# Attention weights turned through two buffers: large query tiles at the end of a turn with transfers of their own, small ones in the next

## The chip, the cores and the metric

The kernel runs on one core of one Trainium2 chip. The metric is the device time of one execution in microseconds (us). PE is the matrix engine (TensorE), PEld its weight loads, DVE is VectorE, ACT ScalarE, POOL GpSimd, and SP is SyncE, which here issues nearly all DMAs.

## What is computed

The reference is a block of three residual steps on an input of 16 batches, 512 tokens and width 256. The first and the last step are a feed-forward part with routed slots, and the middle one, which the change touches, is causal self-attention with 16 heads of width 64 and rotary positions:

```python
x = x + 0.5 * ffn(layernorm(x))
x = x + attn(layernorm(x))
x = x + 0.5 * ffn(layernorm(x))

def attn(x):
    q, k, v = heads(x @ Wq + bq), *heads(split(x @ Wkv + bkv))
    q, k = rope(q), rope(k)
    scores = where(causal, q @ k.T / sqrt(64), -inf)
    return concat(softmax(scores) @ v) @ Wo + bo
```

All is float32.

## The kernel before

Attention works in 64 units: a batch `b` and a group `hg` of four heads. A loop over `u` (L1207) makes one **turn** per step, and each turn works on several units at once: `sums(u)` and `leave(u)` finish unit `u`, `old` is unit `u+1`, whose softmax weights are scaled and turned, `new` is unit `u+2`, whose scores and exponentials are made, and `queries_keys(u+3)` makes the next queries and keys. All engines' orders within attention are written out by hand: every engine runs its instructions in the order in which the loop's calls stand, so a wait of one instruction holds all that stand behind it on the same engine. SP's DMA issues are in this order too.

The 512 queries of a unit are four tiles of 128 (0 to 3). Because of the causal mask, tile `i` has `i+1` blocks of 128 x 128, ten in all. Scores come in three groups: `scores((3,))`, `scores((2,))` early in a turn, `scores((1, 0))` at its end. `exps` (L1061) follows each group: on VectorE a masked copy out of PSUM with the row's minimum (L1073), on ScalarE the exponential with the row's sum (L1077). `scaled` (L1080) takes reciprocals of the sums on VectorE (L1082) and multiplies on POOL (L1085). The weights of tiles 3 and 2 lie in one SBUF tile, `pr0` (7 blocks per head), those of 1 and 0 in another, `pr1` (3 blocks).

To multiply by the values, the weights must stand with their keys on the partitions. This is done in two steps. `turn` (L1088, L1100) transposes every 32 x 32 square of a block on VectorE, from `pr` into `sq`. Then `move` (L1119, L1127) issues 16 DMAs on SP that bring each band of 32 partitions of `sq` to its place in `prT`. `sq` and `prT` are one buffer each: `sq` can be written again when the 16 DMAs have read it, and `prT` when `sums` have read it. `turn_most(j)` turns six of the seven blocks of tiles 3 and 2 for head `j`, `turn_corner` the last one for all heads, `turn_tile(1)` and `turn_tile(0)` the small tiles. For the first unit and the last, `turn_at_once` does the whole on PE instead.

`sums` (L1149, L1158) multiplies: for each pair of heads and each key block `t`, one matmul per head over the `4 - t` query tiles that see it, accumulated in a PSUM bank (`p_av`) that ScalarE then copies to `aoT` (L1169). `leave` (L1171) multiplies by Wo and VectorE adds to the residual (L1182). The q and k products (L988) are biased and rotated on VectorE (L994) and POOL (L999, L1000); `values` makes v (L1010).

In every fourth turn a new batch is entered: ScalarE normalizes it (`enter`, L936), VectorE transposes it (L961), and a `Trip` stores it to DRAM on SP (L964). In the two turns after that, `land` issues eight DMAs each on SP (L970) that read it back turned. In these turns SP also stores a finished batch (L1184, two DMAs).

PSUM has eight banks that go around: in a turn `sums` takes two, scores of tile 3 four, of tile 2 four, `leave` two, q, k and v two each, scores of tiles 1 and 0 four. So the third and fourth head of `scores((2,))` use the banks that the two `p_av` leave, and each group of scores starts with small matmuls of a blank tile (L1047) that are first to wait for a bank.

In a turn of the kernel before, the order around the change is: `sums`; `enter` and `land` where there are any; `scaled` of `old`'s tiles 1 and 0 for two heads, `turn_most(1)`, `turn_most(2)`, `scaled` for the other two heads, `turn_most(3)`, `turn_corner`, `turn_tile(1)`; `scores((3,))`, `scores((2,))`; the exps of tile 3's first head; `turn_tile(0)` and `move`; the other exps; `leave`; statistics, q, k and v; `scores((1, 0))`, `turn_most(0)`, `exps((1, 0))`.

Of the kernel before, what the change touches and what calls it, by code (L numbers as in the profile page):

```python
# [9 lines left out]
F32 = mybir.dt.float32  # L10
# [5 lines left out]
P = 128  # L16
NB, S, D = 16, 512, 256
NT = S // P
# [15 lines left out]
AH, DQ = 16, 64  # L34
HG = 4
NHG = AH // HG
SQ = 32
NSQ = P // SQ
# [9 lines left out]
def macaron_kernel(ctx: ExitStack, tc: tile.TileContext, a: dict, out: bass.AP):  # L48
    nc = tc.nc
# [6 lines left out]
    def ps(name):  # L56
        return psum.tile([P, 512], F32, tag="b", name=name, bufs=8)
# [22 lines left out]
    ident = const.tile([P, P], F32, tag="ident", name="ident")  # L80
# [83 lines left out]
    with tc.tile_pool(name="setup", bufs=1) as su:  # L164
# [3 lines left out]
        sq = su.tile([NS, D], F32, tag="sq", name="sq")  # L168
# [7 lines left out]
        with tc.manual_schedule(engines={mybir.EngineType.DVE, mybir.EngineType.Activation}):  # L176
            pt = ps("p_sqT")
# [20 lines left out]
            for c in range(NC):  # L198
                for k in range(NC):
                    nc.tensor.matmul(pq[:, c * NS:(c + 1) * NS], d_wq[:, k, c * P:(c + 1) * P], sqT[:, k, :],  # L200
                                     start=(k == 0), stop=(k == NC - 1))
# [683 lines left out]
    def attention(qp, wq, wk, wv, wo, cos, sin, row):  # L885


        ap = None
# [23 lines left out]
        hTs, hs, qs, ks, vs, oTs, prTs, stds, trips = {}, {}, {}, {}, {}, {}, {}, {}, {}  # L912
# [30 lines left out]
        def width(b):  # L943
            hTs[b] = qp.tile([P, NC, S], F32, tag="hT", name=f"ahT{b}", bufs=2)
            for c in range(NC):
                pt = ps(f"p_ahT{b}_{c}")
                for t in range(NT):
                    nc.tensor.transpose(pt[:, t * P:(t + 1) * P], hs[b][t // 2][:, t % 2, c * P:(c + 1) * P], ident)
                nc.scalar.copy(hTs[b][:, c, :], pt)  # L949
# [65 lines left out]

        blocks = NT * (NT + 1) // 2
        first = [0, 4, 8, 7]
        place = {0: (1, 0, 1), 1: (1, 1, 2), 2: (0, 0, 3), 3: (0, 3, 4)}  # L1020

        class Weights:

# [2 lines left out]
            def __init__(self, u):  # L1026
                b, hg = units[u]
                self.u, self.hg, self.nm = u, hg, f"{b}_{hg}"
                self.mn = small.tile([P, NT, HG], F32, tag="amn", name=f"amn{self.nm}")
                self.rs = small.tile([P, NT, HG], F32, tag="ars", name=f"ars{self.nm}")  # L1030
                self.pr = [None, None]
                self.banks = {}

            def at(self, i, j):
# [53 lines left out]
            def turn(self, which, heads, of, src, dst):  # L1088

                if heads[0] == 0 and which == 0 and len(of) == 2:
                    self.sq = ap.tile([P, NSQ, HG, blocks * SQ], F32, tag="sq", name=f"sq{self.nm}")
                pr = self.pr[which]

                def view(x, at, dims):
                    return bass.AP(x.tensor, x.offset + at, [list(x.ap[0])] + [[s, n] for s, n in dims if n > 1])
                j, nh = heads
                step = (7, 3)[which] * P
                nc.vector.transpose(  # L1100
                    view(self.sq, j * blocks * SQ + dst[0] * SQ,
                         [(blocks * SQ, nh)] + [(s * SQ, n) for s, (_, n) in zip(dst[1:], of)]
                         + [(HG * blocks * SQ, NSQ), (1, SQ)]),
                    view(pr, j * step + src * P,
                         [(step, nh)] + [(s * P, n) for s, n in of] + [(SQ, NSQ), (1, SQ)]))

            def turn_most(self, j):
                self.turn(0, (j, 1), [(3, 2), (1, 3)], 0, (2, 1, 3))

            def turn_corner(self):  # L1110
                self.turn(0, (0, HG), [], 6, (first[3],))

            def turn_tile(self, i):
                if i:
                    self.turn(1, (0, HG), [(1, 2)], 1, (1, 3))
                else:
                    self.turn(1, (0, HG), [], 0, (0,))

            def move(self):  # L1119

                prT = prTs[self.u] = ap.tile([P, NSQ, HG, blocks * SQ], F32, tag="prT", name=f"prT{self.nm}")
                for n in range(NSQ):
                    for k in range(NSQ):
                        q = (k + n) % NSQ
                        nc.sync.dma_start(prT[k * SQ:(k + 1) * SQ, q, :, :], self.sq[q * SQ:(q + 1) * SQ, k, :, :])  # L1127

            def turn_at_once(self, tag, vector):


                prT = prTs[self.u] = ap.tile([P, NSQ, HG, blocks * SQ], F32, tag=tag, name=f"prT{self.nm}")
                where = {first[t] + i - t: (i, t) for i in range(NT) for t in range(i + 1)}
                per = S // P
                for g in range(HG * blocks // per):
                    pt = ps(f"p_prT{self.nm}_{g}")
                    for n in range(per):
                        j, at = divmod(g * per + n, blocks)
                        i, t = where[at]
                        nc.tensor.transpose(pt[:, n * P:(n + 1) * P], self.at(i, j)[:, t * P:(t + 1) * P], ident)  # L1140
                    dst = prT.rearrange("p a h f -> p a (h f)")[:, :, g * per * SQ:(g + 1) * per * SQ]
                    dst = dst.rearrange("p a (n x) -> p a n x", n=per)
                    src = pt.rearrange("p (n a x) -> p a n x", n=per, a=NSQ)
                    if g in vector:
                        nc.vector.tensor_copy(dst, src)
                    else:
                        nc.scalar.copy(dst, src)

        def sums(u, pair):  # L1149
            b, hg = units[u]  # L1150
            if pair == 0:
                oTs[u] = ap.tile([P, HG // 2, S], F32, tag="oT", name=f"aoT{b}_{hg}")
            po = ps(f"p_av{b}_{hg}_{pair}")
            for t in range(NT):
                n = NT - t
                for j in range(2):
                    head = pair * 2 + j
                    nc.tensor.matmul(  # L1158
                        po[j * DQ:(j + 1) * DQ, :].rearrange("d (a f) -> d a f", a=NSQ)[:, :, t * SQ:],
                        vs[u][:, t, head * DQ:(head + 1) * DQ],  # L1160
                        prTs[u][:, :, head, first[t] * SQ:(first[t] + n) * SQ],
                        start=(t == 0), stop=(t == NT - 1))

            r = R_BV + hg * (HG // 2) + pair
            dst = oTs[u][:, pair, :].rearrange("d (i o a y) -> d o a i y", i=NT // 2, o=2, a=NSQ)
            src = po.rearrange("d (a i o y) -> d o a i y", i=NT // 2, o=2, a=NSQ)
            for odd, to, of in ((1, slice(0, 4), slice(0, 4)), (0, slice(2, 4), slice(0, 2)),
                                (0, slice(0, 2), slice(2, 4))):
                nc.scalar.activation(dst[:, odd, to], src[:, odd, of], AF.Identity, bias=bcol[:, r:r + 1])  # L1169
# [31 lines left out]
        ap = yield [lambda: width(0)] + queries_keys(0)  # L1201
        ws = {}
        seen = 2 * NHG
        with tc.tile_pool(name="awayh", bufs=2, space=bass.MemoryType.DRAM) as away, \
                tc.manual_schedule(engines={mybir.EngineType.DVE, mybir.EngineType.Activation,
                                            mybir.EngineType.Pool, mybir.EngineType.SP}):
            for u in range(-2, nu):  # L1207
                new = ws[u + 2] = Weights(u + 2) if u + 2 < nu else None
                qk = queries_keys(u + 3)
                old = ws.get(u + 1)  # L1210
# [10 lines left out]
                if u >= 0:  # L1221
                    sums(u, 0)
                    sums(u, 1)
# [6 lines left out]
                if old and u + 2 == nu:  # L1230
                    old.turn_at_once("sq", range(0, 10, 2))
                elif u == -1:
                    values(0, 0)
                    values(0, 2)
                    old.turn_at_once("prT", range(2, 10, 3))
                elif old:
                    old.scaled((1, 0), slice(0, HG // 2))
                    old.turn_most(1)
                    old.turn_most(2)
                    old.scaled((1, 0), slice(HG // 2, HG))  # L1240
                    old.turn_most(3)
                    old.turn_corner()
                    old.turn_tile(1)
                if new:
                    new.scores((3,))
                    new.scores((2,))
                    new.exps((3,), slice(0, 1))
                if old and 0 <= u < nu - 2:
                    old.turn_tile(0)
                    old.move()  # L1250
                if new:
                    new.exps((3,), slice(1, 2))
                gone = [leave(u, 0)] if u >= 0 else []
                if fresh == 1:
                    width(1)
# [18 lines left out]
                if u == nu - 1:  # L1274
                    for g in range(PB):
                        entered[g] = xs[g]
                        for t in range(NT):
                            i = (g % PB) * NT + t
# [17 lines left out]
                if new and u > -2:  # L1296
                    new.scores((1, 0))
                    if u + 3 < nu:
                        new.turn_most(0)
                    new.exps((1, 0))  # L1300
            token_stats(NB - 2, NT - 1)
        yield
# [54 lines left out]
```

## Time and profile before

| | us |
|---|---|
| median of three runs | 2309.89 (2309.47 to 2314.15) |
| the profiled execution | 2317.09 |
| its span, first to last instruction | 2315.4 |
| of which attention's steady turns | 476.5 to 1881.8, 60 turns |
| PE busy in the span | 2254.7 (97%) |
| VectorE busy | 1761.6 (76%) |
| all 992 issues of L1127, median of one | 0.59 |

The profile is one execution. An engine is busy while it runs an instruction; an SP row gives the time that SP takes to issue a DMA, not the time that the DMA takes. In a timeline's rows the first number is the start, the second the time from the start of the first to the end of the last of equal neighbours, then engine, line, operation, the tiles written and read, the count, and in brackets the idle time before it and what ended it. A group of matmuls shows twice as many records as the program has matmuls, since one in float32 runs as two. The granted clock of PE was 0.995 over the span.

### The profile page before, as it was taken

How to read it: one execution, taken by the hardware profiler on the slowest of the kernel's cores; microseconds unless marked ns; L12 is line 12 of the kernel's file. 1: busy time of each engine (PE TensorE's matmuls, PEld its weight loads, DVE VectorE, ACT ScalarE, POOL GpSimd, SP SyncE). 2: the span in 40 equal slices, each digit the busy share in tenths (PEclk: the TensorE clock that was granted, in tenths of full speed). 3: DMA queues.
4: the chain of work that ended last, by engine and by line, in shares of the span. 5: the costliest groups of instructions: out<-in, count | busy, mean ns of one | idle time of the engine just before them, and what ended most of it. 6: DMA issues, size and time to landing. Idle time of an engine off the chain costs nothing. (4 is left out here: it accounts for less than half of the span.)

```text
span 2315.4 us, 52884 instructions
## 1 busy us (share of the span) xinstructions
PE 2254.7 (97%) x19544; PEld 1488.2 (64%) x19544; DVE 1761.6 (76%) x4678; ACT 1158.1 (50%) x3296; POOL 1068.6 (46%) x1695
## 2 busy tenths in 40 slices
PE   7999999999999999999999999999999999998999
PEld 4764488566666666666666666666666666764588
DVE  5742298788889898989898988989888875432387
ACT  5753243455555555556464545555555555532233
POOL 2210054565566556565656565656556542210043
PEclk9999999999999999999999999999999999999999
DMA  6839851055556465554655554646455543739734
GB/s 209 261 112 403 339 140 55 7 131 121 130 127 147 110 148 130 122 140 111 146 129 129 128 140 111 158 97 160 120 132 130 124 115 112 237 138 404 305 116 140
DMA packets 221929, 359.52 MB, mean 155 GB/s; under 512 B 99876, under 2 KB 159848, under 8 KB 213480
## 3 DMA queue, kind: packets, MB, share of 16 engines
q1 hardware_dynamic: 220812, 355.34, 55.3%
q8 instruction: 155, 2.54, 0.5%
q14 instruction: 102, 0.84, 0.1%
q10 hardware_dynamic: 860, 0.81, 0.1%
HBM read 156.29 MB, written 37.22 MB: 84 GB/s over the span
## 5 line engine op out<-in xcount | busy, mean ns | idle before, releaser
L1085 POOL TENSOR_SCALAR pr<-pr,ars 128x512 f32<-128x512 f32 (+3 forms) x1024 | 524.1, 532 | 575.0 <-DVE ars L1082 573.8
L1077 ACT ACTIVATE pr<-pr,amn 128x512 f32<-128x512 f32 (+3 forms) x1024 | 561.8, 550 | 219.6 <-DVE amn L1073 215.2
L1100 DVE STREAM_TRANSPOSE sq<-pr 128x768 f32<-128x768 f32 x434 | 384.5, 918 | 130.1 <-DMA prT<-sq 106.7
L1073 DVE CUSTOM_DVE_ANT_0 pr<-p_as,causal 128x512 f32<-128x512 f32 (+2 forms) x768 | 308.6, 457 | 7.0 <-PE p_as L1054 5.8
L1054 PE MATMUL p_as<-k,q 32*64 32x448 f32 (+3 forms) x8192 | 307.3, 414 | 0.0
L1158 PE MATMUL p_av<-prT,v 128*64 128x512 f32 (+3 forms) x2048 | 291.5, 437 | 10.1 <-ACT pr L1077 2.0
L1013 ACT COPY v<-p_v 128x512 f32<-128x512 f32 x128 | 74.6, 585 | 451.3 <-PE p_v L1010 451.3
L1158 PEld LDWEIGHTS p_av<-prT,v 128*64 128x64 f32 x2048 | 161.1, 137 | 139.6 <-issue 92.7
L1176 PE MATMUL p_ay<-wo,aoT 128*128 128x256 f32 x1024 | 238.6, 386 | 4.1 <-DVE amn L1073 3.0
L1010 PE MATMUL p_v<-wv,ahT 128*128 128x256 f32 x1024 | 231.6, 379 | 0.7 <-DVE x L1182 0.7
L988 PE MATMUL p_q<-ahT,wq 128*128 128x512 f32 x512 | 230.6, 593 | 0.2 <-ACT ahT L949 0.2
L1054 PEld LDWEIGHTS p_as<-k,q 32*64 32x64 f32 x8192 | 201.8, 131 | 45.0 <-issue 26.2
L988 PE MATMUL p_k<-ahT,wk 128*128 128x512 f32 x512 | 230.3, 592 | 0.0
L1176 PEld LDWEIGHTS p_ay<-wo,aoT 128*128 128x128 f32 x1024 | 189.2, 190 | 62.2 <-DVE amn L1073 37.0
L1010 PEld LDWEIGHTS p_v<-wv,ahT 128*128 128x128 f32 x1024 | 194.5, 190 | 53.8 <-issue 23.7
L1077 ACT ACTIVATION_READ_ACCUMULATOR pr<-pr,amn 128x1 f32 x1024 | 192.0, 187 | 0.0
L988 PEld LDWEIGHTS p_k<-ahT,wk 128*128 128x128 f32 x512 | 97.3, 190 | 122.0 <-issue 106.9
L988 PEld LDWEIGHTS p_q<-ahT,wq 128*128 128x128 f32 x512 | 97.0, 190 | 95.7 <-issue 78.6
L1073 DVE CUSTOM_DVE_ANT_1 pr<-p_as,causal 128x384 f32<-128x384 f32 x256 | 130.2, 546 | 0.0
L1169 ACT ACTIVATE aoT<-p_av,bcol 128x128 f32<-128x128 f32 (+1 forms) x384 | 117.1, 391 | 9.9 <-PE p_av L1158 9.9
L584 PE MATMUL p_ds<-hT,qk 128*128 128x512 f32 x256 | 118.8, 609 | 2.1 <-ACT hT L159 2.1
L811 PE MATMUL p_cy<-vw,catT 128*128 128x256 f32 x512 | 120.8, 379 | 0.0
(179 smaller groups left out, 3358.0 us busy)
## 6 DMA issues: line engine op xcount, KB each, us to landing
prT<-sq SPq DMA_DIRECT2D x992, 160.0 KB
w<-in_e_W_dram SPq DMA_DIRECT2D x64, 1024.0 KB
w<-in_e_Wg_dram SPq DMA_DIRECT2D x32, 1024.0 KB
out_dram<-x SPq DMA_DIRECT2D x64, 256.0 KB
awaya<-sqa SPq DMA_DIRECT2D x25, 512.0 KB
atT<-awaya SPq DMA_DIRECT2D x100, 128.0 KB
xl<-in_attn_x_dram SPq DMA_DIRECT2D x16, 512.0 KB
xl<-out_dram SPq DMA_DIRECT2D x16, 512.0 KB
```

What stands on the lines that cost most here:

```text
L584: nc.tensor.matmul(psc, qk[:, k, c * P:(c + 1) * P], hT[:, k, :], start=(k == 0), stop=(k == NC - 1))
L811: nc.tensor.matmul(py[:, t * D:(t + 1) * D], atT[:, c, t * P:(t + 1) * P], vws[b][:, c, :], start=(c == 0), stop=(c == NC - 1))
L988: nc.tensor.matmul(pq, self.w[:, k, at:at + P], hTs[self.b][:, k, :], start=(k == 0), stop=(k == NC - 1))
L1010: nc.tensor.matmul(pv[:, t * 256:(t + 1) * 256], hTs[b][:, k, (t0 + t) * P:(t0 + t + 1) * P], wv[:, k, hg * HG * DQ:(hg + 1) * HG * DQ], s ...
L1054: nc.tensor.matmul(banks[j][half * H:(half + 1) * H, at:at + wh], q[n][rows, q0:q0 + H], k[n][rows, :wh], start=(n == 0), stop=(n == 1))
L1073: nc.vector.tensor_tensor_reduce(out=by_block(self.at(i, j)), in0=by_block(banks[j][:, at:at + w]), in1=mask(i), scale=-1.0 / math.sqrt(DQ ...
L1077: nc.scalar.activation(self.at(i, j), self.at(i, j), AF.Exp, bias=self.mn[:, i, j:j + 1], scale=-1.0, accum_out=self.rs[:, i, j:j + 1])
L1085: nc.gpsimd.tensor_scalar(self.at(i, j), self.at(i, j), self.rs[:, i, j:j + 1], 1.0, ALU.mult, ALU.mult)
L1100: nc.vector.transpose(view(self.sq, j * blocks * SQ + dst[0] * SQ, [(blocks * SQ, nh)] + [(s * SQ, n) for s, (_, n) in zip(dst[1:], of)] + ...
L1158: nc.tensor.matmul(po[j * DQ:(j + 1) * DQ, :].rearrange("d (a f) -> d a f", a=NSQ)[:, :, t * SQ:], vs[u][:, t, head * DQ:(head + 1) * DQ], ...
L1169: nc.scalar.activation(dst[:, odd, to], src[:, odd, of], AF.Identity, bias=bcol[:, r:r + 1])
L1176: nc.tensor.matmul(py[:, t * D:(t + 1) * D], oTs[u][:, pair, (t0 + t) * P:(t0 + t + 1) * P], wo[:, hg * (HG // 2) + pair, :], start=(pair ...
```

## The change

The turned weights get two buffers, `sq0`/`prT0` for tiles 3 and 2 (7 blocks per head) and `sq1`/`prT1` for tiles 1 and 0 (3 blocks per head), of the same size together. All of `turn_most` and `turn_corner` now stand at the end of the turn in which tiles 3 and 2 were made, ahead of `exps((1, 0))`; the tiles 1 and 0 are turned in the next turn, after the exps of tile 3's first two heads. `move` is called twice, `move(0)` at the place where the old unit's `scaled` begins, behind `sums` and `land`, and `move(1)` after the small tiles; each issues 16 DMAs. `sums` is split where the buffers are split: six matmuls per head instead of four, over the same ten blocks, first the four on `prT0`, then two on `prT1`.

```diff
-        blocks = NT * (NT + 1) // 2
-        first = [0, 4, 8, 7]
+        blocks = (7, 3)
+        where = ([(2, 0), (3, 0), (2, 1), (3, 1), (2, 2), (3, 2), (3, 3)], [(0, 0), (1, 0), (1, 1)])
+        pieces = [(0, t, max(t, 2), NT - max(t, 2)) for t in range(NT)] + [(1, t, t, 2 - t) for t in range(2)]
...
-            def move(self):
-                prT = prTs[self.u] = ap.tile([P, NSQ, HG, blocks * SQ], F32, tag="prT", name=f"prT{self.nm}")
+            def targets(self, tag, which):
+                if which == 0:
+                    prTs[self.u] = [None, None]
+                n = blocks[which] * SQ
+                prT = prTs[self.u][which] = ap.tile([P, NSQ, HG, n], F32, tag=f"{tag}{which}",
+                                                    name=f"prT{which}_{self.nm}")
+                return prT
+
+            def move(self, which):
+                prT, sq = self.targets("prT", which), self.sq[which]
                 for n in range(NSQ):
                     for k in range(NSQ):
                         q = (k + n) % NSQ
-                        nc.sync.dma_start(prT[k * SQ:(k + 1) * SQ, q, :, :], self.sq[q * SQ:(q + 1) * SQ, k, :, :])
+                        nc.sync.dma_start(prT[k * SQ:(k + 1) * SQ, q, :, :], sq[q * SQ:(q + 1) * SQ, k, :, :])
...
         def sums(u, pair):
...
-            for t in range(NT):
-                n = NT - t
+            for one, (which, t, i, n) in enumerate(pieces):
+                at = where[which].index((i, t))
                 for j in range(2):
                     head = pair * 2 + j
                     nc.tensor.matmul(
-                        po[j * DQ:(j + 1) * DQ, :].rearrange("d (a f) -> d a f", a=NSQ)[:, :, t * SQ:],
+                        po[j * DQ:(j + 1) * DQ, :].rearrange("d (a f) -> d a f", a=NSQ)[:, :, i * SQ:(i + n) * SQ],
                         vs[u][:, t, head * DQ:(head + 1) * DQ],
-                        prTs[u][:, :, head, first[t] * SQ:(first[t] + n) * SQ],
-                        start=(t == 0), stop=(t == NT - 1))
+                        prTs[u][which][:, :, head, at * SQ:(at + n) * SQ],
+                        start=(one == 0), stop=(one == len(pieces) - 1))
...
                 elif old:
+                    old.move(0)
                     old.scaled((1, 0), slice(0, HG // 2))
-                    old.turn_most(1)
-                    old.turn_most(2)
                     old.scaled((1, 0), slice(HG // 2, HG))
-                    old.turn_most(3)
-                    old.turn_corner()
-                    old.turn_tile(1)
                 if new:
                     new.scores((3,))
                     new.scores((2,))
-                    new.exps((3,), slice(0, 1))
+                    new.exps((3,), slice(0, 2))
                 if old and 0 <= u < nu - 2:
+                    old.turn_tile(1)
                     old.turn_tile(0)
-                    old.move()
-                if new:
-                    new.exps((3,), slice(1, 2))
+                    old.move(1)
...
                     new.scores((1, 0))
                     if u + 3 < nu:
-                        new.turn_most(0)
+                        for j in range(HG):
+                            new.turn_most(j)
+                        new.turn_corner()
                     new.exps((1, 0))
```

`turn` and `turn_at_once` are changed only in which buffer they write.

## The prediction

> **What bounds the kernel now.** I read the page's engine shares first, then the busy time of the attention's steady turns (476.5 to 1881.8 us, 60 turns). The page's chain reaches back only into the last part of the kernel, so for attention I went by TensorE's and SyncE's timelines.
>
> ```profile
> PE 2254.7 (97%) x19544; PEld 1488.2 (64%) x19544; DVE 1761.6 (76%) x4678; ACT 1158.1 (50%) x3296; POOL 1068.6 (46%) x1695
> ```
> ```profile
> 476.50:1881.80 1405.30, 1393.36 (x13448) 887.92 (x13448) 1248.63 (x3433) 767.92 (x2490) 831.96 (x1260) 1.00 0.55 130
> ```
>
> In these 60 turns PE is idle for 1405.3 - 1393.4 = 11.9 us, at a granted clock of 1.00. A turn takes 1405.3 / 60 = 23.42 us.
>
> ```profile
> 1015.33 4.53 PE L1158 MATMUL p_av<-prT,v 128*64 128x512 f32 x32
> ...
> 1023.20 3.72 PE L1176 MATMUL p_ay<-wo,aoT 128*128 128x256 f32 x16 [0.20 <-DVE amn L1073]
> 1026.75 3.60 PE L988 MATMUL p_q<-ahT,wq 128*128 128x512 f32 x8
> 1030.19 3.60 PE L988 MATMUL p_k<-ahT,wk 128*128 128x512 f32 x8
> 1033.62 3.62 PE L1010 MATMUL p_v<-wv,ahT 128*128 128x256 f32 x16
> ...
> 1038.93 4.53 PE L1158 MATMUL p_av<-prT,v 128*64 128x512 f32 x32
> ```
>
> From `sums` to `sums` this turn took 23.60 us. The shortest turns of the timeline take 23.25, and the surplus sits in the scores just before `leave`. So PE sets the pace, and nothing can win much more than 11.9 us.
>
> ```profile
> DVE sq L1100 <- DMA prT<-sq: 106.7, 52, 3.1
> ```
> ```profile
> 1037.65 0.98 DVE L1100 STREAM_TRANSPOSE sq<-pr 128x768 f32<-128x768 f32 x1 [2.05 <-DMA prT<-sq]
> ...
> 1038.78 0.42 DVE L1073 CUSTOM_DVE_ANT_0 pr<-p_as,causal 128x256 f32<-128x256 f32 x1
> ...
> 1039.30 0.51 ACT L1077 ACTIVATE pr<-pr,amn 128x256 f32<-128x256 f32 x1 [1.44 <-DVE amn L1073]
> ...
> 1042.83 1.82 ACT L1169 ACTIVATE aoT<-p_av,bcol 128x256 f32<-128x256 f32 x6
> ...
> 1043.03 0.13 DVE L1082 RECIPROCAL ars<-ars 128x4 f32<-128x4 f32 x1
> ...
> 1045.18 0.21 PE L1047 MATMUL p_as<-blank 32*64 32x64 bf16 x3
> ...
> 1045.73 0.65 DVE L1073 CUSTOM_DVE_ANT_0 pr<-p_as,causal 128x512 f32<-128x512 f32 x1
> ```
>
> VectorE waits about 2 us a turn for the move, but it only uses up slack: exps((1,0)) start at 1038.78, ScalarE ends theirs at 1042.83 and the copies out of p_av at 1044.65. The latter free the PSUM banks that scores((2,)) need on PE at 1045.18: half a microsecond to spare.
>
> ```profile
> 1011.62 0.51 SPq L964 DMA_DIRECT2D away<-ahT  x1
> 1012.24 1.57 SPq L1184 DMA_DIRECT2D out_dram<-x  x2
> 1016.06 4.85 SPq L970 DMA_DIRECT2D ahT<-away  x8
> 1023.83 10.05 SPq L1127 DMA_DIRECT2D prT<-sq  x16
> 1033.92 5.37 SPq L970 DMA_DIRECT2D ahT<-away  x8
> ```
> ```profile
> L1127 SPq DMA_DIRECT2D prT<-sq x992: 507/590/1704, 460.3 to 1899.5; - x199
> ```
>
> SyncE issues the 16 moves of a turn one after another: 10.05 us, which is 15 steps of 0.635 and a last issue of about 0.5 to 0.6. For 160 KB every 0.635 us the DMA engines are no limit yet.
>
> **The change part by part.**
>
> *Matmuls of `sums`.* 24 instead of 16 per turn, over the same 10 blocks of 128 columns per head. The 32 records take 4.46 us to the next matmul (1015.33 to 1019.79), 0.11 per 128 columns of two heads side by side; p_v's records of 256 columns take 0.22 each (3.55/16), and p_catT's of 128 0.11 (0.44/4). Cost goes by columns. Bounds: 0, or 16 more loads of 137 ns wholly exposed, 2.2 us a turn. I take 0: in the present run of 128-column pieces the loads already hide.
>
> *VectorE.* The same seven transposes per turn (0.87 a step for each of the four large ones, 0.62 corner, 1.17 and 0.63 for the tiles). They move: four large and the corner now stand together before exps((1,0)), 4.1 us instead of 0.87; the wait for the old move goes, since sq0 is read early in a turn. Both reciprocals now come before exps((3,)), so VectorE waits for ScalarE to end exps((1,0)), 4.25 us after their start (1038.78 to 1043.03); this is still before scores((3,)) are done, so it costs nothing itself. `turn_tile(1)` waits for POOL's products of tile 1, some 1.5 us after the second reciprocal, 5.8 after exps((1,0)) began; VectorE gets there 7.6 into the turn. `turn_most` waits until `move(0)` has landed, some 16 into a turn, and is due at 20.6. Neither costs anything; 0.6 of slack is the smaller cover.
>
> *SyncE and DMA.* The bytes stay; 32 DMAs instead of 16, with rows of 3584 and 1536 bytes instead of 5120. Engines are 0.55 busy and have room. The queue has not: 32 issues at 0.635 are 20.3 us of a 23.4 us turn, beside 16 landings, two outputs and one trip per four turns. And `move(0)` now stands behind the landings and waits for `sums` of the same turn to be done with prT0, while the next `sums` wants prT1 after its first 7 blocks. That closes a loop:
>
> - `sums` release prT0 to the first issue 0.06 (as 1047.03 to 1047.09 now), one first step 0.56 and 30 of 0.635: the last issue starts after 19.67.
> - That DMA lands 1.97 later (completion records: median of the last of eight landings ahT<-away, 32 KB each; the first move of a turn, 160 KB, takes 2.47). PE wakes 0.06 later: 21.7.
> - PE then does 3 blocks of pair 0 and 7 of pair 1 before prT0 is free again: 10 x 0.215 + 0.17 of pipeline = 2.3. The loop takes **24.0 us**, 0.58 over a turn now.
> - After each of the 14 trips SyncE also issues L964, waits until it has landed, and issues 8 landings (4.0) before `move(0)`. From L964 to L970 it is 4.44 here (1011.62 to 1016.06) and 2.68 where the queue is quiet (130.84 to 133.52, awaya to atT); between them 3.5. `move(0)` starts 20.3 + 3.5 + 4.0 = 27.85 after the last release instead of 24.0: **3.85** late (3.0 to 4.8). The outputs' two issues lie inside that wait, and the other landings in the 3.7 us between the last move and the release.
>
> Sum over 61 turns between moves: 61 x 0.58 + 14 x 3.85 = 35 + 54 = +89 us.
>
> The unknown price is the spacing of the smaller moves. Above: 0.635, the row of the same 32-row form. Below: 0.47 (four atT<-awaya in 1.74) and 0.49 (ahT<-away), of other forms. At 0.49 the loop takes 19.5 us and is hidden. I take 0.635, since rows with less data (128-byte pieces) are not far cheaper than large ones and the form is unchanged, and keep both ends.
>
> [...]
>
> **The rivals.**
>
> *Cheap issues; VectorE and ScalarE bind (30%).* If the spacing falls under about 0.6, the late exps decide. From exps((3,)) to the last k product VectorE takes 13.05 us (1045.73 to 1058.78); with tile 1, four large ones and the corner 13.05 + 1.17 + 4.1 = 18.3. Scores((3,)) are done 6.4 into a turn, so exps((1,0)) start at 24.7, 1.46 into the next turn; 5.9 later (1038.78 to 1044.65) p_av's banks are free, at 7.35, and PE wants them at 6.25. It loses 1.1, which gives the next turn its slack back: 0.55 a turn. In turns with a trip, two more transposes (1.3) raise the wait to 2.5, so four turns lose some 0 + 2.5 + 0 + 1.2 = 3.7, less 0.7 that they lose now: 3.0 x 15.25 = +46, 2356 us (2335 to 2385). In my forecast this wait falls in the time that PE stands at `sums` anyway.
>
> *Faster (6%).* Issues are cheap and the transposes of a turn's end go into VectorE's former waits, so that exps((1,0)) start less than 0.3 us into a turn; then PE's idle time goes, at most 11.9: 2298. The point is that 18.3 would have to be under 17.1. Only the 106.7 us of waits speak for it.
>
> *Nothing measurable (5%).* The two chains sit just under PE's 23.25, within 4.6 us (0.2%, about what a measurement here can tell from no change).
>
> *Worse (5%).* Landings and the new waits add up beyond the loop: over 2425.
>
> **How the numbers follow.** The sum stands against the profiled execution, 2317.1 us (span 2315.4): 2406. The median of the runs is 7.2 lower, which makes 2399. Its own range, with 3.0 to 4.8 per trip and 0.3 either way in the loop: 2375 to 2425, chance 54%. The range 2335 to 2425 takes in the cheap-issue rival and leaves out 16%. Faster by over 0.2%: 6%; within 0.2%: 5%; slower: 89%.
>
> **What would show it.** Right: SyncE issuing almost without pause; PE idle before L1158's later pieces, ended by DMA prT1; turns of 24, and some of 28 after a trip; VectorE's waits for moves gone. Cheap issues instead: spacing of 0.5, PE idle before scores ended by ACT aoT, and SyncE waiting for PE between `move(1)` and `move(0)`. Wrong altogether: turns of 23.25. Should `sums` itself take over 4.6 us without a wait, the loads were mis-costed.

## The result and the profile after

The changed kernel takes 2536.93 us (median of four runs, 2528.88 to 2543.04), the kernel before beside it 2311.05. The ratio is 1.097, with a 95% interval of 1.094 to 1.101: 226 us slower, where the prediction said 2399 us, 88 slower, and at most 2425. The direction was right and the size was not. The profiled execution took 2538.9 us, its span is 2537.1.

First the page's busy time of the engines and the attention's 60 steady turns, in the columns shown before (us, then busy time by engine, granted clock, DMA share and GB/s):

```profile
PE 2326.8 (92%) x20568; PEld 1596.9 (63%) x20568; DVE 1762.2 (69%) x4678; ACT 1165.9 (46%) x3296; POOL 1069.5 (42%) x1695
```
```profile
476.50:2101.70 1625.20, 1467.17 (x14405) 994.07 (x14401) 1248.13 (x3430) 775.72 (x2490) 832.76 (x1260) 0.95 0.47 112
```

The 60 turns now take 1625.2 instead of 1405.3 us, 27.1 a turn. Nearly the whole loss is here. PE was idle for 11.9 us of them and is idle for 158 now. But its *busy* time rose as well, by 73.8 us, for the same multiplications, and the granted clock fell from 1.00 to 0.95. The prediction has no term for that.

Next the groups of the page for `sums` and for the transposes (count, busy and mean; then the idle time before them and what ended it), and the waits of SyncE's queue:

```profile
L1170 PE MATMUL p_av<-prT,v 128*64 128x256 f32 (+1 forms) x3072 | 368.7, 398 | 163.2 <-DMA prT<-sq 150.1
...
L1103 DVE STREAM_TRANSPOSE sq<-pr 128x768 f32<-128x768 f32 x434 | 370.4, 908 | 1.8 <-DMA prT<-sq 1.8
```
```profile
SPq L1138 <- PE p_av L1170: 162.5, 46, 5.9
```

VectorE's waits for the move are gone (106.7 to 1.8), as foreseen. In their place TensorE waits 150 us for prT inside `sums`, and SyncE waits 162 us for `sums` to release prT0: each waits for the other, which is the loop of the prediction. All other parts of a turn keep their length (scores 3.05, `leave` 3.56, q and k 3.43, v 3.55); `sums` went from 4.46 to 8.16 us on average.

One turn on PE, then four rows of SyncE's queue around a trip:

```profile
1036.01 1.73 PE L1170 MATMUL p_av<-prT,v 128*64 128x256 f32 x16
1039.99 4.72 PE L1170 MATMUL p_av<-prT,v 128*64 128x256 f32 x32 [2.25 <-DMA prT<-sq]
```
```profile
1040.70:1044.20 3.50, 3.50 (x24) 2.56 (x21) 0.18 (x1) 1.65 (x7) 2.60 (x7) 0.51 0.00 0
```
```profile
959.06 21.82 SPq L1138 DMA_DIRECT2D prT<-sq  x32
980.98 0.53 SPq L964 DMA_DIRECT2D away<-ahT  x1
...
984.16 3.78 SPq L970 DMA_DIRECT2D ahT<-away  x8
988.05 22.17 SPq L1138 DMA_DIRECT2D prT<-sq  x32
```

The first 16 records of `sums` take 1.73 us. Then PE waits 2.25 us for prT1, and the other 32 records take 4.72, where they take 3.03 at full clock (e1 below). The window over them (second fence: PE busy throughout, clock 0.51) tells why: from 1040.73 on, for 3.41 us, the trace has a granted clock of 0.5. `sums` release prT0 only near the end of this slow stretch (the next `move(0)` begins at 1043.89), so it lies on the loop: SyncE issues `move(0)` later, prT1 lands later, PE waits again, and the clock is at 0.5 again (from 1068.03 and from 1095.34). In SyncE's rows the trip stands where it was expected, with L964, 3.2 us from it to the first landing, and eight landings between two moves, but 32 issues take 21.8 and 22.2 us there, where the prediction had 20.3.

Taken apart by the trace's single records, from the first issue of one `move(0)` to the next (mean of 60 turns, 27.16 us):

| term of the loop | predicted | measured |
|---|---|---|
| first to last of 32 issues | 19.61 | 20.98 |
| landing, and PE awake | 2.03 | 2.19 |
| PE to the release of prT0 and SyncE awake, 46 turns without a trip | 2.36 | 3.46 (2.41 at full clock) |
| the same, 14 turns with a trip | 2.36 + 3.85 = 6.21 | 5.73 (5.1 to 5.6 in eight, 6.2 to 6.5 in the six with a landing that took over 1 us to issue) |

In the last row SyncE's own queue sets the time and not PE: SyncE waits for `sums` 46 times (the row of waits above), as often as there are turns without a trip. The differences account for the miss: 60 x 1.37 = 82 us for the issues, 60 x 0.16 = 10 for the landing, 46 x 1.10 = 51 for the multiplications and 14 x -0.48 = -7 for the trips. That is 136 us beside the forecast's 89, together 225.

### The profile page after: what moved, and what is told of

Same layout as the page of the kernel before. It is cut to its first block, busy times and chain, and to the rows that moved or that the text cites. A ratio compares the mean times of both kernels' runs of the same rounds, so it can differ in the third digit from the quotient of the medians.

```text
span 2537.1 us, 56418 instructions
## 1 busy us (share of the span) xinstructions
PE 2326.8 (92%) x20568; PEld 1596.9 (63%) x20568; DVE 1762.2 (69%) x4678; ACT 1165.9 (46%) x3296; POOL 1069.5 (42%) x1695
## 5 line engine op out<-in xcount | busy, mean ns | idle before, releaser
L1170 PE MATMUL p_av<-prT,v 128*64 128x256 f32 (+1 forms) x3072 | 368.7, 398 | 163.2 <-DMA prT<-sq 150.1
L1170 PEld LDWEIGHTS p_av<-prT,v 128*64 128x64 f32 x3072 | 266.4, 159 | 264.0 <-issue 176.8
L1103 DVE STREAM_TRANSPOSE sq<-pr 128x768 f32<-128x768 f32 x434 | 370.4, 908 | 1.8 <-DMA prT<-sq 1.8
L1056 PEld LDWEIGHTS p_as<-k,q 32*64 32x64 f32 x8192 | 208.5, 131 | 42.7 <-issue 23.5
L1181 ACT ACTIVATE aoT<-p_av,bcol 128x128 f32<-128x128 f32 (+1 forms) x384 | 123.2, 395 | 129.3 <-PE p_av L1170 129.0
L1084 DVE RECIPROCAL ars<-ars 128x4 f32<-128x4 f32 x254 | 44.9, 177 | 118.6 <-ACT pr L1079 106.9
```

The costliest lines, as they stand in the source:

```text
L1056: nc.tensor.matmul(banks[j][half * H:(half + 1) * H, at:at + wh], q[n][rows, q0:q0 + H], k[n][rows, :wh], start=(n == 0), stop=(n == 1))
L1103: nc.vector.transpose(view(sq, j * n + dst[0] * SQ, [(n, nh)] + [(s * SQ, m) for s, (_, m) in zip(dst[1:], of)] + [(HG * n, NSQ), (1, SQ)] ...
L1170: nc.tensor.matmul(po[j * DQ:(j + 1) * DQ, :].rearrange("d (a f) -> d a f", a=NSQ)[:, :, i * SQ:(i + n) * SQ], vs[u][:, t, head * DQ:(head ...
```

## The experiments

Each was measured beside the kernel before on the same chip.

| run | what it is | us | ratio to before (95%) |
|---|---|---|---|
| e1_warm | changed kernel, 1.5 us more work for PE ahead of the wait | 2520.06 | 1.089 (1.087 to 1.092) |
| e2_order | changed kernel, sums buffer by buffer | 2443.86 | 1.056 (1.054 to 1.058) |
| e3_few | changed kernel, `move(1)` in 4 DMAs | 2351.03 | 1.017 (1.015 to 1.018) |
| e4_trip | changed kernel, trips issued by ScalarE | 2544.80 | 1.100 (1.098 to 1.103) |
| e5_split | kernel before, sums in 24 matmuls | 2317.27 | 1.002 (1.001 to 1.003) |
| e6_old32 | two buffers and 32 issues, VectorE's old order | 2527.91 | 1.092 (1.091 to 1.094) |
| e7_old20 | e6 with `move(1)` in 4 DMAs | 2302.24 | 0.995 (0.994 to 0.997) |
| e8_diag_after | changed kernel, 24 issues, POOL copies the rest | 2466.51 | 1.067 (1.065 to 1.069) |
| e9_diag_old | e6, 24 issues, POOL copies the rest | 2302.72 | 0.996 (0.995 to 0.997) |
| e10_diag_before | kernel before, 12 issues, POOL copies the rest | 2299.72 | 0.995 (0.993 to 0.996) |
| e11_diag_after2 | e8 with the copies placed later | 2368.35 | 1.024 (1.022 to 1.025) |
| e12_land2 | changed kernel, 16 landings of a trip in 4 DMAs | 2466.16 | 1.065 (1.063 to 1.068) |

**e1_warm: is it the clock?** Pair 0's seven blocks of prT0 are multiplied twice.

```diff
-            for one, (which, t, i, n) in enumerate(pieces):
+            again = [(one, one == len(pieces) - 1, piece) for one, piece in enumerate(pieces)]
+            if pair == 0 and u < nu - 2:
+                again = [(one, one == NT - 1, piece) for one, _, piece in again[:NT]] + again
+            for one, done, (which, t, i, n) in again:
...
-                        start=(one == 0), stop=(one == len(pieces) - 1))
+                        start=(one == 0), stop=done)
```

> Pair 0 does its seven blocks of prT0 twice, the second time from a fresh start, so TensorE has 7 x 0.215 = 1.5 us more work ahead of its wait for prT1 and the result is the same. Theory A (the wait lets the granted clock fall, and the half-speed records then stand in the loop): of the 61 waits of over 0.3 us in the changed kernel none of those under 1.9 us was followed by a half-clock stretch, 38 of the 43 longer ones were. With 1.5 us filled, ordinary waits of 1.3 to 3.1 become 0 to 1.6, their stretches go, and about 16 ordinary turns win 1.5 us each, though TensorE does more: 2510 us (2490 to 2522). The longer waits behind a trip keep theirs. Theory B (the clock only falls along with the wait and costs nothing of its own, or the added work stands in the loop): 2537 to 2630.

Measured: 2520.06 us, 17 less than the changed kernel, with intervals that do not overlap and inside theory A's range, although PE does 992 records, that is 496 matmuls, more. (The counts in the expectation are off: the changed kernel's trace has 39 waits of PE of 1.95 us or more, 34 of them with a half-clock stretch, not 43 and 38.) The page and one turn on PE:

```profile
PE 2379.0 (94%) x21560; PEld 1652.7 (66%) x21560; DVE 1762.4 (70%) x4678; ACT 1166.4 (46%) x3296; POOL 1073.1 (43%) x1695
```
```profile
1036.83 3.25 PE L1173 MATMUL p_av<-prT,v 128*64 128x256 f32 x32
1041.03 3.03 PE L1173 MATMUL p_av<-prT,v 128*64 128x256 f32 x32 [0.95 <-DMA prT<-sq]
```

The wait shrank to 0.95 us and the 32 records behind it take 3.03 us again. The half-clock stretches of the 60 turns fell from 33 (146.8 us) to 13 (61.4), the granted clock there rose from 0.95 to 0.98, and each of those left is in the turn behind a trip. Theory A holds. That the gain is 17 us and not 27 is in part the added work itself: in ten turns no wait is left and `sums` take 5.99 us, which is 4.48 and the added 1.5. The span is shorter with more work on the busiest engine (2521.6 us against 2537.1): the clock's share is a cost of its own here.

**e2_order: is it the loop?** Both pairs do their prT0 pieces first, then both their prT1 pieces, and ScalarE's copies out of p_av come behind all of them.

```diff
...
+            for buffer in range(2):
+                for pair, po in enumerate(pos):
+                    for one, (which, t, i, n) in enumerate(pieces):
+                        if which != buffer:
+                            continue
...
```

> Both pairs do their prT0 blocks first and then both their prT1 blocks, so prT0 is free 3.1 us into a turn whether or not prT1 has landed. Theory A (the turn is the loop from prT0's release over 32 issues and a landing back to the release): the loop is cut; prT1 is there 3.1 + 20.9 + 2.2 = 26.2 after a turn's sums began, due at 23.3 + 3.1 = 26.4; what is left is the queue's own load, per four turns 4 x 21.0 for the moves, 16 landings 10, two outputs and L964 some 2 and part of its 3.5 us wait: 24 to 25 a turn, 2365 to 2415 us, and few half-clock stretches. Theory B (the queue is simply too full, and the order within the sums does not matter): 2480 to 2540. Theory C (the copies out of p_av come later and scores wait for their banks): turns of 23.3 plus waits ended by ACT aoT.

Measured: 2443.86, 93 us less than the changed kernel, and 29 more than the top of theory A's range. The loop was worth 93 us, which refutes B; but what is left costs more than expected. Its ordinary turns take some 24.5 us, 29 of them with `sums` at 4.48 and no wait, turns with a trip 26 to 31, and twelve half-clock stretches are left. SyncE's queue is simply full:

```profile
964.03 4.73 SPq L970 DMA_DIRECT2D ahT<-away  x8
968.87 21.03 SPq L1138 DMA_DIRECT2D prT<-sq  x32
989.95 4.18 SPq L970 DMA_DIRECT2D ahT<-away  x8
994.24 15.97 SPq L1138 DMA_DIRECT2D prT<-sq  x24
```

From 964.0 to 1010.2, nearly two turns, there is no pause. Theory C is there too: PE waits 19.4 us for p_av's banks.

**e3_few: is it the number of issues?** The same bytes, 12 issues a turn less. The exchange of quadrants (bands of 32 partitions) in `move(1)` is left out.

```diff
+                if which == 1:
+                    for k in range(NSQ):
+                        nc.sync.dma_start(prT[k * SQ:(k + 1) * SQ], sq[k * SQ:(k + 1) * SQ])
+                    return
```

> move(1) brings the same bytes in 4 DMAs instead of 16, without the exchange of quadrants between partitions (that part of the turning is left out). Theory A (the number of issues is the price, at 0.635 us each): 20 issues take 12.7 us, prT1 is there long before its piece, and turns fall to 23.3 to 23.7: 2300 to 2330 us. Theory B (bytes or the splitting in two buffers are the price): 2450 to 2540. Theory C (with cheap issues the late transposes delay exps((1,0)) and TensorE waits for p_av's banks at the scores): 2356 us, with PE idle before the scores ended by ACT aoT.

Measured: 2351.03 us. Theory B is refuted: with the same bytes and buffers 186 us go. Theory A's mechanism holds, but the number is C's, 2356, which is the rival of the prediction. PE's waits in attention are now nearly all of this kind (us in all, times, longest):

```profile
PE p_as L1049 <- ACT aoT L1185: 25.2, 45, 0.8
```

The waits stand ahead of the scores, where ScalarE's copies out of p_av have to free the banks. The four turns from one trip to the next take 23.5, 24.3, 23.9 and 24.9 us in one round.

**e4_trip: can another queue take the trips?** L964 and L970 are issued by ScalarE (`nc.scalar.dma_start` for `nc.sync.dma_start` in both).

> L964 and the landings L970 are issued by ScalarE instead of SyncE. Theory A (after each of 14 trips SyncE waits for L964 and issues 8 landings ahead of move(0), 3.8 us late): these turns lose the 3.8, and the half-clock stretches of 6.8 us in the sums behind them go: 53 to 85 us less, 2450 to 2485, ordinary turns as before at 25 to 27.5. Theory B (the trips cost only what the clock makes of them, or their issues hide): 2515 to 2540. Theory C (ScalarE's issues hold up its exps): slower than 2540.

Measured: 2544.80, no better than the changed kernel; the intervals overlap. Theory A's number failed. The landings no longer stand ahead of `move(0)`, but now they run beside it (13 issues of SyncE, and the last six of eight of ScalarE):

```profile
1022.43 10.59 SPq L1138 DMA_DIRECT2D prT<-sq  x13
```
```profile
1024.71 4.18 ACTq L970 DMA_DIRECT2D ahT<-away  x6
```

Thirteen of SyncE's issues take 10.6 us instead of 8.2. Its fourth began at 1024.26 and its fifth at 1027.41, with no semaphore wait between, while ScalarE issued. Sixteen times more than 2.1 us pass from one issue to the next inside a move, 14 of them with issues of ScalarE in that time or the microsecond before; in the changed kernel it is never so long. So the 32 issues take 21.8 us on average instead of 21.0. The half-clock stretches stayed at 33. Taken apart like the changed kernel, a gain and a loss nearly cancel: the terms from PE's waking to the next `move(0)` are some 37 us shorter over the 60 turns, the issues some 47 us longer. The time is in theory C's range, but PE shows no wait for ScalarE's work, so not for C's reason.

**e5_split: the matmuls alone.**

```diff
+            pieces = [(t, max(t, 2), NT - max(t, 2)) for t in range(NT)] + [(t, t, 2 - t) for t in range(2)]
+            for one, (t, i, n) in enumerate(pieces):
...
```

> The kernel before with its sums in 24 matmuls instead of 16, six pieces per pair and head as in the changed kernel, everything else as before. Theory A (cost goes by columns, loads hide): no change, 2308 to 2316 us. Theory B (each of the 16 more loads a turn is exposed at 0.137 us): 2.2 us a turn, 2445.

Measured: 2317.27, 1.0017 times before (1.0007 to 1.0026), some 4 us more and 1 us above theory A's range. `sums` take 4.48 instead of 4.46 us a turn, 1.2 us of the 4. The eight more matmuls a turn are nearly free; theory B, 134 us, is refuted.

**e6_old32 and e7_old20: the buffers without the new order.** VectorE's order is that of before, with `move(0)` behind the corner; e7 has `move(1)` in 4 DMAs besides, without the exchange of quadrants.

```diff
-                    old.move(0)
                     old.scaled((1, 0), slice(0, HG // 2))
+                    old.turn_most(1)
+                    old.turn_most(2)
                     old.scaled((1, 0), slice(HG // 2, HG))
+                    old.turn_most(3)
+                    old.turn_corner()
+                    old.move(0)
+                    old.turn_tile(1)
...
-                        for j in range(HG):
-                            new.turn_most(j)
-                        new.turn_corner()
+                        new.turn_most(0)
```

> The changed kernel's two buffers and 32 moves, with VectorE in the order of before (three large tiles, the corner and the small tiles within the turn, move(0) behind the corner and move(1) behind the last small tile). Theory A (the price is 32 issues in a row of 20.9 us, and they start some 6.6 us into the turn): prT1 lands 29 us after the turn's sums began, 4 us after its piece is due, plus the half clock behind such waits: turns of 27 to 29, 2540 to 2640 us, no better than the changed kernel. Theory B (the loop over the release of prT0 behind the wait for prT1 is the price, not the number of issues): 2330 to 2420.

> The run e3 (move(1) in 4 DMAs, without the exchange of quadrants between partitions, which is left out) with VectorE in the order of before. Theory A (the 38 us that e3 still loses are the late exps((1,0)) behind four large transposes and the corner): turns of 23.3 to 23.5, 2305 to 2322 us. Theory B (they are the price of the two buffers or of the four more issues): 2340 to 2360.

Measured: e6 2527.91, 12 us under theory A's range and 9 under the changed kernel, so the new order of VectorE and SyncE gains nothing over the old one. Its mean turn is 26.99 us with 28 half-clock stretches; from the first issue of `move(0)` to the next it shows the same terms (20.7, 2.1 and 4.1). e7 2302.24: theory A. 58 of 60 turns take 23.27 to 23.32. So the 49 us between e3 and e7 are the four large transposes and the corner ahead of exps((1,0)); two buffers with few issues are even 10 us better than before, here without the exchange (e9 below has it).

**e8_diag_after, e11_diag_after2: fewer issues with the whole turning.** In each move the four squares on the diagonal stay on their partitions. GpSimd copies them, and SyncE issues 12 DMAs.

```diff
-                for n in range(NSQ):
+                for n in range(1, NSQ):
                     for k in range(NSQ):
...
+                for k in range(NSQ):
+                    nc.gpsimd.tensor_copy(prT[k * SQ:(k + 1) * SQ, k], sq[k * SQ:(k + 1) * SQ, k])
```

> The changed kernel, but the 4 of each move's 16 squares that stay on their partitions are copied by GpSimd (32x896 and 32x384, 4 each a turn), so SyncE issues 24 DMAs a turn instead of 32 and the whole turning is done. Theory A (the number of issues closes the loop): 8 x 0.635 + the long ones among them = 5.5 us come off a loop of 24.8 to 27.4, it is hidden, and the late exps((1,0)) bind as in e3: 2340 to 2365 us, almost no half-clock stretches. Theory B (something that the quadrants' exchange itself costs): 2450 or more. GpSimd's eight copies, some 0.9 and 0.4 us each by its row of 0.53 for 512 columns, are 5.3 us a turn; if they hold up its additions for q and k, scores((1,0)) wait and it is 2365 to 2420.

Measured: 2466.51; A and the guess for slow copies missed, and the number lies in B's range. But the timeline of POOL shows another loop, which the edit had made:

```profile
1029.01 3.83 POOL L1140 COPY prT<-sq 32x896 f32<-32x896 f32 x4 [3.92 <-PE p_av L1172]
1032.94 3.22 POOL L1087 TENSOR_SCALAR pr<-pr,ars 128x256 f32<-128x256 f32 x8
```

The copies stood in `move(0)`, ahead of the products `scaled((1,0))`. They wait for `sums` to release prT0, and the products, which had been ready, wait behind them. e11 puts the copies behind `move(1)`.

> Run e8 once more, with GpSimd's copies behind its products scaled((1,0)) and behind the last small tile instead of ahead of them; in e8 the copies of move(0) waited on GpSimd for the sums' release of prT0 (208 us in all) and kept the products waiting behind them. Theory A (the number of issues closes the loop; without it the late exps((1,0)) bind, as in e3): 2340 to 2365 us. Theory B (two buffers with late transposes cost 2466 whatever the queues do): 2440 to 2480.

Measured: 2368.35, 3 us over theory A's range. `sums` take 4.48 us again, turns of 24.0 to 24.6 but for two, and PE waits for `ACT aoT` ahead of the scores (36.1 us, 63 times). Theory B is refuted: with the whole turning, eight issues less a turn bring 169 us back, and what remains is the late exps.

**e9_diag_old, e10_diag_before: a version that beats both?** The same copies in e6, and in the kernel before.

> Run e6 (two buffers, VectorE in the order of before) with the same copies on GpSimd: 24 DMAs a turn, whole turning. Theory A: move(0) from 6.6 us into the turn, 24 issues of 15.9 with a long one, landed at 24.7, due at 25: turns of 23.3, as e7: 2300 to 2312 us. Theory B (it just misses, or GpSimd's copies hold up q and k): 2320 to 2400.

> The kernel before with the same copies (four of 32x1280 on GpSimd, some 1.3 us each) and 12 DMAs a turn instead of 16. Theory A (TensorE's last 12 us of waits come from VectorE's wait of 2 us a turn for the move): the move ends 2.5 us earlier, the wait goes: 2300 to 2308 us. Theory B (GpSimd's copies end later than the DMAs did, or hold up q and k): 2312 to 2345.

Measured: 2302.72 and 2299.72, both as theory A had it, and both compute the whole. The kernel before gains 0.54% (0.42 to 0.67) by four issues less and four copies on an engine that had time:

```profile
476.50:1845.70 1369.20, 1361.85 (x13193) 873.31 (x13192) 1233.42 (x3358) 751.72 (x2433) 1105.92 (x1472) 1.00 0.42 103
```
```profile
L1129 POOL COPY prT<-sq x248: 1239/1247/1257, 456.9 to 1881.1; 32x1280 f32<-32x1280 f32 x124
```

PE is idle for 7.4 us in this stretch, nearly all turns take 23.25 to 23.34, and no wait of VectorE for a move is left. The copies cost POOL 1.25 us each, and in attention no wait of TensorE is put down to them.

**e12_land2: the trips.** Each trip's landings are 4 DMAs of 32 partitions instead of 16, without the exchange of quadrants.

```diff
-                    for a in range(NSQ):
-                        nc.sync.dma_start(
-                            hTs[self.b][k * SQ:(k + 1) * SQ].rearrange("y c s -> y (c s)").rearrange(
-                                "y (n a x) -> a y n x", n=n, a=NSQ)[a],
-                            self.mem[a * SQ:(a + 1) * SQ, k * n * SQ:(k + 1) * n * SQ].rearrange(
-                                "y (n x) -> y n x", n=n))
+                    nc.sync.dma_start(hTs[self.b][k * SQ:(k + 1) * SQ].rearrange("y c s -> y (c s)"),
+                                      self.mem[k * SQ:(k + 1) * SQ, :])
```

> The changed kernel with each trip's 16 landings as 4 DMAs of the same bytes in all, without the exchange of quadrants between partitions (that part of the turning is left out). Theory A (after a trip the wait for L964 and 8 issues stand ahead of move(0), 3.8 us beyond the 3.7 of slack): with 2 issues instead of 8 the lateness is 3.5 + 1.0 - 3.7 = 0.8, so 14 x 3.0 = 42 us go, and up to 30 more with the long half-clock stretches behind these waits: 2462 to 2495 us. Theory B (trips cost by the bytes they bring): 2525 to 2540.

Measured: 2466.16, in theory A's range. It is 71 us less, with 17 half-clock stretches, all of 3.41 us, instead of 33. Taken apart as above, some 40 us of it come off the trips' own term, 24 off the multiplications in the other turns and 11 off the issues. So the issues ahead of `move(0)` were the trips' price, and the half clock in the turns behind them added to it.

## Why the prediction was wrong in size

**Right.** PE set the pace, so a turn could only get longer. The median issue of the smaller moves takes 0.59 us and the median step is 0.635, at 112 KB as at 48 KB. The price is the issue, not the bytes: e3 takes 186 us away with the same bytes. The loop was real: cutting it in e2 brought 93 us. The trip was nearly right too: from the last move's issue to the next `move(0)` the prediction has 27.85 - 19.67 = 8.2 us, and it took 7.5 to 7.8 in eight turns and 8.2 to 8.6 in the six with a long landing issue; e12 confirms what it consists of. The matmuls' price of nothing was right to 4 us (e5). The new order's price of nothing was right only in the shadow of `sums`' wait, as the prediction said: uncovered, it costs 49 us (e3 against e7), and the 2356 us worked out for that rival stand against 2351.

**Wrong, the first step.** "One first step 0.56 and 30 of 0.635: the last issue starts after 19.67." The median issue is as stated, but one or two a turn take 1.0 to 2.0 us. The row of before that the prediction quoted says so in its maximum, 1704 ns, and the changed kernel's says it again:

```profile
L1138 SPq DMA_DIRECT2D prT<-sq x1984: 507/590/2042, 452.9 to 2127.8; - x199
```

In the 60 turns 99 issues of SyncE took over 0.8 us, 88.6 us more than the median issue; 86 of them were moves. In the 60 turns of before there were 48, 21 of them moves, and PE was idle for 11.9 us in all. The 32 issues of a turn stand one behind another, so the loop paid their mean and not their median: 20.98 instead of 19.61, 82 us. The prediction's example turn of before (10.05 us for 16) had no long issue in it.

**Wrong, the second step.** "PE then does 3 blocks of pair 0 and 7 of pair 1 before prT0 is free again: 10 x 0.215 + 0.17 of pipeline = 2.3." At full clock that is what it takes (2.41). But this work comes directly behind a wait of PE, and the forecast loop itself makes PE wait, so its speed behind a wait was part of the question. The prediction took the durations of a kernel that never waits there. Measured: 2.41 at full clock, 3.8 to 4.1 with a stretch of 3.41 us at half, 4.57 with one of 6.83; 51 us in the turns without a trip. The trace of before showed the price already: PE's only two long waits at the edges of attention (1.83 us at 455.2, with 0.68 more close behind, and 1.95 us at 1902.5) were each followed by 3.41 us at 0.5.

The traces also show which waits the half clock followed. In those of before and of the changed kernel the granted clock changes only at whole multiples of 3.413 us from one another (the stretches that begin at 1040.73, 1068.03 and 1095.34 are eight such steps apart). Counted in these windows of 3.413 us over the 60 turns, the half clock followed each of the changed kernel's 31 full-clock windows in which PE was idle for 2.06 us or more, two of the five with 1.96 to 2.01, and none of the 396 with less than 1.9. In the 60 turns of before no window has more than 0.29 us of idle time, and the clock stays at 1.00. The five waits of the changed kernel, 2.02 to 3.44 us long, that had no stretch behind them lay across a window's edge, with at most 2.01 us in either window. So whether such a wait was followed by the half clock depended on where it fell, which is luck.

**The range.** Its upper end, 2425, took 0.3 us either way in the loop. Both errors went the same way, and the loop passed each on in full, so 1.37 + 0.16 + 1.10 in a turn without a trip fell outside.

Not settled: what makes an issue long. In the changed kernel each of the 99 long issues ran beside a 16 KB packet of the instruction queue (q8), of which these turns had 115. The trace of before agrees as far as moves go (21 of 21 long ones), but other long issues, such as its 13 stores, had no such packet beside them. It remains a coincidence in time, which no run varied. That SyncE's issues came later while ScalarE issued is seen in e4's pauses (up to 3.15 us from one to the next), without a cause.

## What to carry to other kernels

Count the issues of a DMA queue as an engine's busy time: where splitting transfers filled the queue, as here, the split was paid in full, at the mean issue and not the median (20.98 us a turn against 19.61), even with DMA engines that were busy less than half of the time (0.47). Before taking a wait of TensorE as its own length, look at what TensorE does right after it and whether the next wait depends on that; half-speed work inside the loop was paid here in every round in which it came (4.72 us for 32 records instead of 3.03). And when an engine with time to spare can move the part of the data that stays on its partitions, that can take issues off the queue for nothing (e10, 0.54% faster with four issues less a move), if the copies don't stand ahead of work that others wait for (e8, 2466.51 us against 2368.35 in e11).

## What the runs showed of the hardware

- The granted clock fell to 0.5 behind short waits of TensorE: of 39 waits of 1.95 us or more in the changed kernel's attention 34, of 21 separate ones of 0.3 to 1.9 us none. The stretches lasted 3.41 or 6.83 us, and began 2.1 to 5.1 us after the wait began. In one of them 32 records took 4.72 us that took 3.03 at full clock (e1).
- In the traces of before and of the changed kernel the clock changed only at whole multiples of 3.413 us from one another. Of the changed kernel's full-clock windows of this length in the 60 turns, those with 2.06 us or more of idle time of TensorE were followed by one at half (31 of 31), those with less than 1.9 never (0 of 396). Its windows at half were followed by another with 0.79 us or more of idle time (10 of 10) and by full clock with 0.62 or less (33 of 33).
- A move between partitions of SBUF took SyncE 0.59 us to issue (median) and 0.63 to 0.64 from one to the next, at 48 and 112 KB in the changed kernel as at 160 KB before.
- In the changed kernel 99 of 99 long issues (1.5 us on average instead of 0.59) lay beside a 16 KB packet of the instruction queue (q8).
- While ScalarE issued eight landings (e4), up to 3.15 us passed between two issues of SyncE, and 13 issues took 10.6 us instead of 8.2.
- GpSimd copied 1280 fp32 columns on 32 partitions in 1.25 us (e10, median of 248).
